# Order of projection, old MLP part and v, and where the second norm's rows are turned, in an adaLN transformer block

## The chip, the cores and the metric

The kernel runs on one core of one Trainium2 chip. Its time is device time in microseconds (us). The figure for the kernel before is the median of three runs. The engines are TensorE (PE in the profile; its weight loads are PEld), VectorE (DVE), ScalarE (ACT) and GpSimd (POOL); SyncE (SP) issues nearly all transfers here and computes nothing.

## The reference

One transformer block with adaptive layer norms, float32, for 8 sequences of 1024 tokens and D = 512, 16 heads of 32, causal attention, an MLP of width 2048:

```python
mod = silu(condition) @ Wada + bada
sh_a, sc_a, gt_a, sh_m, sc_m, gt_m = split(mod, 6, axis=1)
xn = layernorm(x, g1, be1)                                    # first norm
xm = xn * (1 + sc_a) + sh_a
x  = x + gt_a * (softmax(causal(q k^T / sqrt(32))) v @ Wproj + bproj)   # q, k, v from xm @ Wqkv
xn = layernorm(x, g2, be2)                                    # second norm
xm = xn * (1 + sc_m) + sh_m
return x + gt_m * (gelu(xm @ W1 + b1) @ W2 + b2)              # exact gelu
```

## The kernel before, in words

**Blocks and windows.** The 8192 tokens are 16 blocks of 512 rows, two a sequence; even blocks are first halves, odd ones second halves (whose attention also reads the keys and values of the half before, so it is longer). The whole kernel is one TensorE program. Attention runs block after block (`attend`). Between its matmuls the planner puts *linear work*: everything else that uses TensorE. The linear work that is to run beside block w's attention is a list of steps, `plan[w]` (the dictionary at L231 and the loop behind it); the text calls this window w. In window w, n = w - 1 is the block whose attention has just ended. Its steps are:

- `v`, `k`, `q`: the values of block w, and the keys and queries of block w + 1;
- `proj`: the output projection of block n, `project_out`. It has four tiles of 128 rows, each a sum over four 128-wide pieces of the attention's output ("steps" of a tile, in the order of the quarters of heads), with Wproj's four pieces as moving data. VectorE multiplies each tile by the gate, GpSimd or VectorE adds it to the residual rows `xr`, and then the second norm's statistics are started (`normalize`);
- `mt`: the second norm's modulation and transposition for block n (key `m`n in `modulated`, L695); `at`: the first norm's for block w + 2 (key `a`n); `load_xa`, `norm_a`: load and normalisation of that block's rows; `load_xr`: load of the rows that the residual is added to; `rows`: broadcast of gate rows;
- `u0` to `u3`: the four parts of the up projection of block n with its gelu (`up`), and `d0` to `d3`: the four parts of the down projection (`down`, L1144). The text calls d0 to d3 the first to the fourth MLP part. The parts that a window doesn't reach stay over for the next one (`late`): d2 and d3, or d1 to d3.

All linear products except the projection are done by a Strassen scheme with seven products of 256-wide halves, so each step ends in additions and subtractions on VectorE and GpSimd (`combine_out`, L193, and `either`, L158). In the second and third MLP part these give `y`, `u_d` and `v_d`; `settle` then applies the gate and adds to the residual. Before a Strassen product, differences of the halves of its input are formed (`T1` to `T4`, for `xm` at L753 and L755).

For windows 3 to 14 the order before is: late parts of block w - 2, v of block w, projection of block n, `mt`, k and q of block w + 1, u0 to u3 and d0 of block n; where w is odd, d1 and the next `at` follow in the same window. So a window after an odd one begins with d2, d3, and a window after an even one with d1, `at`, d2, d3. The two statements that matter are L253 and L263:

```python
steps = late + [("v", w)] + rows_a + [("proj", n), ("mt", n), ("k", w + 1)]
...
late = m[5:6] + at + m[6:]
```

(`m[5:6]` is d1, `m[6:]` is d2 and d3; the second statement is that of even w.) Windows 1, 2 and 15 have orders of their own.

**Turning rows.** A norm's rows lie with tokens on the partitions, and the products want features there. `by_pe` (L375) says which norms are turned on TensorE: before, all second norms, and the first norms of blocks 0 and 1. There each block takes 16 transposes of 128x128 into a PSUM bank (L735), and the modulation (scale and shift of 128x512, L739 on VectorE or L745 on ScalarE, whichever the planner holds to be free sooner) reads the bank. The other 14 first norms ("turned blocks") go another way (`turn`, L663): four VectorE transposes of 32x32 squares (L671) from the `hat` tile, which holds the normalised rows, into `xm`; one SyncE transfer of `xm` to a DRAM tile `held` (L680); four SyncE transfers back into the `hat` tile (L685), which put the squares in place; then modulation from `hat` into `xm`. There is one buffer for `hat` (`hat_tile`, L378), loaded by `load_x` for first norms.

**Attention.** For each quarter g of the heads (four heads) of a block: score units (TensorE `sc`, mask and maximum on VectorE, L1553 and L1556), weights units (`st`: minus the row maximum, then k q^T again; exponential on ScalarE into `pT`), and probabilities-times-v units (`po`). `finish` (L1682) ends a quarter: the sums of the probabilities by a product with ones (L1693), copies of sums and product to SBUF on ScalarE (`rec`, L1702, and `top`), four reciprocals of 128 columns each on VectorE (`invert`, L1711), and one multiplication on GpSimd (`quotient`, L1736), which writes the quarter's part of the attention's output over the queries `qT`. The projection of a block reads all four quarters; its last operand is that of g = 3.

**What sets the order.** Nothing is scheduled at run time: while the program is built, a planner keeps a clock for each engine (`now`), adds an estimated duration for each instruction, and keeps due times of values (`written`, `left`). Linear work runs in threads: the main one walks the plan, side threads hold what was started beside it (`at`, `mt`, tails of Strassen products). `work` advances the thread that waits least by those clocks; `step_aside` decides whether attention or linear work is next. Small jobs of VectorE, ScalarE and GpSimd (reciprocals, transposes of 32x32 squares, statistics) wait in lists and are put out once the clocks say that they are due; jobs of a second norm and of the last quarter stand first in VectorE's list. A DRAM transfer of `turn` is reckoned at 8 us each way (`HOLDING`). `costs` holds 16 transposes for each `at` and `mt`; `planned_time` makes of it the pace at which linear work is spread over a window's attention. The order so found on each engine is then fixed, and engines wait for one another by semaphores.

**Weights** come through a ring of eight SBUF tiles, in the order of the plan (`order`, `fetch`), by transfers on SyncE, which takes its instructions in order; a piece is fetched once the tile eight pieces before is released. The held tile's transfers are in the same queue.

Of the kernel before, what the change touches and what calls it, by code (L numbers as in the profile page):

```python
# [22 lines left out]
def kernel(  # L23
# [42 lines left out]
    NC = D // P  # L66
# [24 lines left out]
    NB = len(blocks)  # L91
# [3 lines left out]
    written, left = {}, {}  # L95
    shape = [None]
    pool_spans = []
    NEVER = float("inf")
# [38 lines left out]
    def note_act(ns, func, reads=(), writes=()):  # L137
        if func is not None and table[0] != func:
            table[0] = func
            ns += TABLE  # L140
        note("ACT", ns, reads, writes)

    def sooner(reads, writes, dve, act):

        t = due(reads, writes)
        return "DVE" if max(now["DVE"], t) + dve <= max(now["ACT"], t) + act else "ACT"
# [81 lines left out]
    def mlp_steps(n):  # L228
        return [("u", n, i) for i in range(NQ)] + [("d", n, part) for part in range(4)]
# [8 lines left out]
    late = []  # L238
    for w in range(1, NB):
        n = w - 1  # L240
        m = mlp_steps(n)
        even = blocks[n][1] == 0
        rows_a = [("rows", blocks[n][0], "a")] if even else []
        rows_m = [("rows", blocks[n][0], "m")] if even else []
        own = m[:1] + ([("load_xa", w + 2)] if w + 2 < NB else []) + m[1:3]
        own += [("norm_a", w + 2)] if w + 2 < NB else []
        if w == NB - 1:
            steps = late[:1] + rows_a + [("proj", n), ("mt", n)] + late[1:]
            steps += [("v", w)] + rows_m + own + m[3:5] + [("load_xr", w)] + m[5:6]
            late = m[6:]  # L250
        else:

            steps = late + [("v", w)] + rows_a + [("proj", n), ("mt", n), ("k", w + 1)]  # L253
            if w == 2:
                steps = late + [("v", w), ("k", w + 1)] + rows_a + [("proj", n), ("mt", n)]
            if w == 1:
                steps = rows_a + [("k", w + 1), ("proj", n), ("mt", n)]
            steps += [("q", w + 1)] + rows_m + own
            at = [("at", w + 2)] if w + 2 < NB else []
            if blocks[w][1] == 0:  # L260

                steps += m[3:5] + [("load_xr", w)]
                late = m[5:6] + at + m[6:]  # L263
            else:
                steps += m[3:5] + [("load_xr", w)] + m[5:6] + at
                late = m[6:]
        plan[w] = steps
    n = NB - 1
# [99 lines left out]
    at, r0 = [], 0  # L368
# [3 lines left out]
        r0 += n  # L372
    O_G1, O_BE1, O_G2, O_BE2, O_BPROJ, O_B2, O_B1, O_BADA = at

    by_pe = {f"m{n}" for n in range(NB)} | {"a0", "a1"}  # L375
    Q = P // NTT

    def hat_tile(key):  # L378
        return tmp.tile([P, NTT, D], F32, tag="hat", name=f"hat_{key}", bufs=1)

    def load_x(n):
        b, h = blocks[n]
        rows = hat_tile(f"a{n}")
        for t in range(NTT):
            some = x[b, h * TB + t * P : h * TB + (t + 1) * P, :]
            if f"a{n}" in by_pe:
                nc.sync.dma_start(rows[:, t, :], some)
            else:
                nc.sync.dma_start(rows[ts(t, Q), :, :], some.rearrange("(t i) d -> i t d", i=Q))
        return rows  # L390
# [145 lines left out]
    act_jobs = []  # L536
# [43 lines left out]
    def normalize(tiles, key, sources):  # L580

        for t in range(NTT):
            written["hat", key, t] = NEVER
        mv = small.tile([P, NTT, 2], F32, tag="mv", name=f"mv_{key}")
        rstd = small.tile([P, NTT], F32, tag="rstd", name=f"rstd_{key}")
        offset = small.tile([P, NTT], F32, tag="offset", name=f"offset_{key}")

        def statistics(t):
            st = small.tile([P, nc.vector.BN_STATS_DIM], F32, tag="st", name=f"st_{key}_{t}")
            nc.vector.bn_stats(st, tiles[:, t, :])  # L590
            nc.vector.bn_aggr(mv[:, t, :], st)
            note("DVE", 850, [sources[t]], [("mv", key)])
            if t < NTT - 1:
                return
            if alone[0]:
                root()
                for i in range(NTT):
                    apply_tile(i)
                return
            power()  # L600
            for i in range(NTT):
                act_jobs.append((lambda i=i: apply_tile(i), [("rstd", key)]))

        def root():
            nc.scalar.activation(rstd, mv[:, :, 1], AF.Sqrt, bias=eps)
            note_act(300, "sqrt", [("mv", key)], [("rstd", key)])
            nc.vector.reciprocal(rstd, rstd)
            nc.vector.scalar_tensor_tensor(offset, mv[:, :, 0], -1.0, rstd, ALU.mult, ALU.mult)
            note("DVE", 360, [("rstd", key)], [("rstd", key)], port=True)

        def power():
            nc.gpsimd.tensor_scalar(rstd, mv[:, :, 1], EPS, None, ALU.add)
            nc.gpsimd.tensor_tensor(rstd, rstd, minus_half, ALU.pow)
            nc.gpsimd.tensor_scalar(offset, mv[:, :, 0], -1.0, None, ALU.mult)
            nc.gpsimd.tensor_tensor(offset, offset, rstd, ALU.mult)
            note("POOL", 1500, [("mv", key)], [("rstd", key)])

        to = [None]

        def apply_tile(t):  # L620
            if t == 0:
                hats[key] = to[0] = hat_tile(key) if key[0] == "m" else tiles
            xh, xt = to[0][:, t, :], tiles[:, t, :]
            reads, writes = [("rstd", key)], [("hat", key, t)]
            if (key == "a0" and t % 2) if alone[0] else sooner(reads, writes, 700, 800) == "DVE":
                nc.vector.tensor_scalar(
                    xh, xt, rstd[:, t : t + 1], offset[:, t : t + 1], ALU.mult, ALU.add
                )
                note("DVE", 700, reads, writes, port=True)
            else:  # L630
                nc.scalar.activation(
                    xh, xt, AF.Identity, bias=offset[:, t : t + 1], scale=rstd[:, t : t + 1]
                )
                note_act(800, None, reads, writes)

        for t in range(NTT):
            add_job(lambda t=t: statistics(t), [sources[t]], key[0] == "m")
# [54 lines left out]
    def modulated(key, gain, shift, b, guards):  # L692
# [22 lines left out]
        at = {t: (key, t) for t in part}  # L715
        if turned:
            yield from turn(key, got, xm)
        for c in range(NC):
            if turned:
                if c:  # L720
                    yield [("turned", key)], []
                source, out = ("turned", key), xm[:, c, :].rearrange("p (a x) -> p a x", x=P)
                values = got[:, :, ts(c, P)]
                if key[0] == "m":
                    out = xm[:, c, :].rearrange("p (t a x) -> p t a x", t=2, a=NTT)
                    values = values.rearrange("p a (t x) -> p t a x", t=2)
            else:
                if c:
                    yield [("hat", key, 0)], [BANK]
                bank = lin_bank()  # L730
                source, out, values = ("l", bank), xm[:, c, :], banks[bank]
                for t in range(NTT):
                    if t:
                        yield [("hat", key, t)], []
                    nc.tensor.transpose(banks[bank][:, ts(t, P)], got[:, t, ts(c, P)], ident)  # L735
                    note_pe(TR, "whole", [("hat", key, t)], [("l", bank)])
            writes = [at["B11"], at["T1"]] if c < 2 else [at["B21"], at["B22"]]
            if sooner([source], writes, 770, 780) == "DVE":
                nc.vector.tensor_scalar(  # L739
                    out, values, gain[:, c, b : b + 1], shift[:, c, b : b + 1],  # L740
                    ALU.mult, ALU.add,
                )
                note("DVE", 770, [source], writes, port=turned)
            else:
                nc.scalar.activation(  # L745
                    out, values, AF.Identity,
                    bias=shift[:, c, b : b + 1], scale=gain[:, c, b : b + 1],
                )
                note_act(780, None, [source], writes)
            if not turned:  # L750
                live[bank] = False
            if c == 1:
                nc.vector.tensor_tensor(part["T1"], part["T1"], part["B11"], ALU.subtract)  # L753
                note("DVE", 700, [at["B11"], at["T1"]], [at["T1"]], port=True)
# [258 lines left out]
    def project_out(n):  # L1013
# [46 lines left out]
        if not last:  # L1060
            normalize(residual[n], f"m{n}", [("xr", n, t) for t in range(NTT)])
# [877 lines left out]
```

## Time and profile before

| | us |
|---|---|
| median of three runs | 3546.27 |
| lowest, highest | 3541.39, 3548.40 |
| the profiled execution, its own time | 3542.2 |
| its span (first to last instruction) | 3540.5 |

The profiled execution's mean granted TensorE clock is 0.998. A profile page gives busy time of each engine and its share of the span; then the span in 40 slices, the DMA queues, and the chain of work that ended last. After that come groups of instructions: source line, engine, operation, output<-inputs (by the program's names, buffer numbers left out) with partitions x elements, count | busy us, mean ns of one | idle time of that engine just before them and what ended most of it. Four views of the trace are used besides:

- The timeline: start in us, duration in us, engine, line, operation, operands, count (x4: four in a row, the duration is that of all four), and in brackets the idle time ahead with what ended it, where there is any. SPq is SyncE's queue.
- Waits: engine, tile and line, <- what ended the wait, then the total in us, how many, and the longest in us.
- Windows: the stretch A:B in us, its length, then busy time and number of instructions for TensorE, weight loads, VectorE, ScalarE and GpSimd, the granted clock, the DMA share and GB/s.
- One tile's or one line's instructions: count, duration in ns (shortest/median/longest), start of the first and of the last in us, forms.

### The profile page before, as it was taken

Reading aid. Unit: us, or ns where it says so; the run is one execution under the profiler, and the core shown is the slowest. Engines: PE = TensorE matmul, PEld = TensorE weight load, DVE = VectorE, ACT = ScalarE, POOL = GpSimd, SP = SyncE. Lnnn points to the kernel's source line nnn. Section 1 sums busy time; section 2 is a strip of 40 time slices with the busy share of each in tenths; the row PEclk is TensorE's granted clock in tenths of the full one; section 3 lists DMA queues with packets and bytes.
Section 4 is the critical chain, followed back from the end, with each engine's and each line's share of the span. In section 5 each row is a group of like instructions: output and inputs, shape, how many; then the busy total and the mean of one; then the engine's idle time right before and its main releaser. Section 6 shows DMA issues by size and latency. Waiting matters only on the chain.

```text
span 3540.5 us, 120499 instructions
## 1 busy us (share of the span) xinstructions
PE 3482.5 (98%) x54621; PEld 1738.0 (49%) x54621; DVE 2174.2 (61%) x2383; ACT 1190.1 (34%) x1237; POOL 2074.9 (59%) x2249
## 2 busy tenths in 40 slices
PE   8999999999999999999999999999999999999999
PEld 4444445445554555545554454544545445454445
DVE  5776675564756557565675656656566556655563
ACT  2334323352333513235232342323423234232521
POOL 2667836666376664666546675366762667526660
PEclk9999999999999999999999999999999999999999
DMA  6753434335443354524445334443344533443334
GB/s 198 245 163 103 137 117 140 111 111 156 117 148 103 110 160 117 168 85 126 142 118 159 103 115 141 124 149 107 118 132 127 156 106 119 135 126 124 100 110 140
DMA packets 319555, 465.96 MB, mean 132 GB/s; under 512 B 26300, under 2 KB 176636, under 8 KB 316996
## 3 DMA queue, kind: packets, MB, share of 16 engines
q1 hardware_dynamic: 318928, 458.22, 42.9%
q8 instruction: 430, 7.05, 0.8%
q14 instruction: 81, 0.66, 0.1%
q10 hardware_dynamic: 116, 0.03, 0.0%
HBM read 412.99 MB, written 43.06 MB: 129 GB/s over the span
## 4 chain that ended last, share of the span: by engine, by line
PE 88%; DMA 4%; DVE 3%; POOL 2%; issue 1%; ACT 1%; SPq 0%; ACTq 0%; DVEq 0%; POOLq 0%
PE bank L202 61%; PE sc L1541 8%; PE po L1672 7%; PE st L1632 7%; PE st L1620 3%; DMA w<-in_L_cond_Wproj_dram 2%; PE bank L1693 2%; PE bank L735 1%; DVE mx L1556 1%; POOL pT L1762 1%; DMA w<-in_L_cond_Wada_dram 1%; PE bank L1594 0%; POOL hT L161 0%; POOL xr L161 0%; DVE sc L1553 0%
## 5 line engine op out<-in xcount | busy, mean ns | idle before, releaser
L1762 POOL TENSOR_TENSOR pT<-pT,pT 128x256 f32<-128x256 f32 (+3 forms) x1254 | 1207.2, 998 | 347.9 <-PE po L1672 181.4
L1644 ACT ACTIVATE pT<-st 128x2048 f32<-128x2048 f32 x288 | 541.0, 1879 | 1000.5 <-PE st L1632 883.3
L202 PE MATMUL bank<-w,hT 128*32 128x256 f32 x14336 | 812.3, 380 | 1.1 <-ACT rec L1702 0.9
L1556 DVE TENSOR_REDUCE mx<-sc 128x4 f32<-128x2048 f32 (+3 forms) x384 | 666.0, 1755 | 197.7 <-PE sc L1541 191.6
L202 PEld LDWEIGHTS bank<-w,hT 128*32 128x32 f32 x14336 | 450.4, 110 | 369.2 <-issue 81.4
L202 PE MATMUL bank<-xm_m,w 128*32 128x256 f32 x8192 | 499.6, 381 | 0.0
L202 PE MATMUL bank<-t_m,w 128*32 128x256 f32 x6144 | 381.2, 380 | 0.0
L1649 POOL TENSOR_SCALAR_AFFINE_SELECT pT<-pT 128x512 f32<-128x512 f32 x256 | 168.8, 677 | 346.6 <-ACT pT L1644 344.2
L202 PEld LDWEIGHTS bank<-xm_m,w 128*32 128x32 f32 x8192 | 255.7, 110 | 224.7 <-issue 62.4
L1553 DVE TENSOR_TENSOR sc<-sc,mask 128x1024 f32<-128x1024 f32 (+1 forms) x160 | 162.9, 1018 | 319.7 <-PE sc L1541 242.5
L1541 PE MATMUL sc<-kT,qT 32*128 32x512 f32 (+3 forms) x3072 | 329.1, 520 | 1.8 <-DVE mx L1556 1.1
L1672 PE MATMUL po<-pT,v 128*32 128x512 f32 (+3 forms) x3048 | 302.9, 492 | 2.0 <-POOL pT L1649 2.0
L1632 PE MATMUL st<-qT,kT 32*128 32x512 f32 (+3 forms) x3072 | 301.0, 487 | 0.0
L202 PEld LDWEIGHTS bank<-t_m,w 128*32 128x32 f32 x6144 | 190.0, 110 | 173.3 <-issue 48.5
L202 PE MATMUL bank<-xm_a,w 128*32 128x256 f32 x3968 | 249.3, 382 | 0.0
L202 PE MATMUL bank<-w,qT 128*32 128x512 f32 x2048 | 238.2, 594 | 8.7 <-DMA w<-in_L_cond_Wproj_dram 7.2
L1711 DVE RECIPROCAL rec<-rec 128x128 f32<-128x128 f32 x256 | 225.7, 920 | 31.5 <-ACT rec L1702 31.5
L1541 PEld LDWEIGHTS sc<-kT,qT 32*128 32x128 f32 x3072 | 129.3, 183 | 179.3 <-issue 73.0
L193 DVE TENSOR_TENSOR hT<-bank,u_u 128x512 f32<-128x512 f32 x192 | 129.9, 687 | 114.1 <-PE bank L202 107.4
L202 PE MATMUL bank<-t_a,w 128*32 128x256 f32 x2944 | 188.4, 382 | 0.4 <-ACT xm_m L745 0.4
L1069 ACT ACTIVATE hT<-hT,cols 128x512 f32<-128x512 f32 x256 | 164.4, 711 | 35.5 <-DVE hT L193 35.0
L202 PEld LDWEIGHTS bank<-xm_a,w 128*32 128x32 f32 x3968 | 122.7, 110 | 105.5 <-issue 32.6
(216 smaller groups left out, 3384.6 us busy)
## 6 DMA issues: line engine op xcount, KB each, us to landing
w<-in_L_cond_W_dram SPq DMA_DIRECT2D x384, 256.0 KB
w<-kept_up_S SPq DMA_DIRECT2D x256, 256.0 KB
w<-kept_down_S SPq DMA_DIRECT2D x256, 256.0 KB
w<-kept_qkv_S SPq DMA_DIRECT2D x180, 256.0 KB
w<-in_L_cond_Wqkv_dram SPq DMA_DIRECT2D x147, 256.0 KB
hat_a<-in_x_dram SPq DMA_DIRECT2D x64, 256.0 KB
xr<-in_x_dram SPq DMA_DIRECT2D x32, 512.0 KB
w<-in_L_cond_Wproj_dram SPq DMA_DIRECT2D x64, 256.0 KB
```

The costliest lines, as they stand in the source:

```text
L193: nc.vector.tensor_tensor(out, src, other, op)
L202: nc.tensor.matmul(ps[r, :], columns, rhs, start=start, stop=stop, skip_group_check=True)
L1069: nc.scalar.activation(hT[:, i, :], hT[:, i, :], AF.Gelu, bias=cols[:, O_B1 + f : O_B1 + f + 1])
L1541: nc.tensor.matmul(sc[:, j, c0 : c0 + w], qTs[n][r, gg, ts(qt, P)], keys_of(n, kh)[r, gg, :w], start=True, stop=True, skip_group_check=True,)
L1553: nc.vector.tensor_tensor(place, place, shape_of.to_broadcast(place.shape), ALU.add)
L1556: nc.vector.tensor_reduce(maxima[n, gg][:, kh, qt, :], sc[:, :, c0 : c0 + w], axis=AX.X, op=ALU.max)
L1632: nc.tensor.matmul(st[:, j, c0 : c0 + w], kT[r, gg, ts(k % NTT, P)], qT[r, gg, TB - w :], start=False, stop=True, skip_group_check=True,)
L1644: nc.scalar.activation(pT[:, :, :used], st[:, :, :used], AF.Exp, scale=scale)
L1649: nc.gpsimd.affine_select(diagonal, diagonal, pattern=[[0, HPG], [1, P]], compare_op=ALU.is_ge, fill=0.0, base=0, channel_multiplier=-1,)
L1672: nc.tensor.matmul(po[r, TB - w :], v[:, k % NTT, g * P + j * hd : g * P + (j + 1) * hd], pT[:, j, c0 : c0 + w], start=(k == 0), stop=last ...
L1711: nc.vector.reciprocal(some, some)
L1762: nc.gpsimd.tensor_tensor(into, into, pT[:, j, c0 : c0 + w], ALU.add)
```

## The change

There are three edits.

The order of windows 3 to 14: the late parts without the last one, then the projection of block n and `mt`, and only then d3 of the block before (`late[-1:]`) and v of block w, before k and q. The projection so stands ahead of d3 and v, not behind them. For even blocks w the late list now begins with `at` and not with d1: `[at, d1, d2, d3]`.

Who turns the second norm's rows: `by_pe` keeps only `a0`, `a1`, `m0`, `m14` and `m15`. The second norms of blocks 1 to 13 go through `turn`: four VectorE transposes, `held` in DRAM and back. Two branches that were in the kernel before are thereby used: in `modulated`, the values of a turned second norm are written with the tokens in another order within each half of 256, and `down` reads the columns of the hidden layer in an order that makes up for it.

The `hat` tile is held apart: `load_x` marks it as taken, the last modulation of a first norm marks it free, and the planner puts out the normalisation of a second norm's rows only then.

```diff
--- before.py
+++ after.py
@@ -250,7 +250,7 @@
             late = m[6:]
         else:
 
-            steps = late + [("v", w)] + rows_a + [("proj", n), ("mt", n), ("k", w + 1)]
+            steps = late[:-1] + rows_a + [("proj", n), ("mt", n)] + late[-1:] + [("v", w), ("k", w + 1)]
             if w == 2:
                 steps = late + [("v", w), ("k", w + 1)] + rows_a + [("proj", n), ("mt", n)]
             if w == 1:
@@ -260,7 +260,7 @@
             if blocks[w][1] == 0:
 
                 steps += m[3:5] + [("load_xr", w)]
-                late = m[5:6] + at + m[6:]
+                late = at + m[5:]
             else:
                 steps += m[3:5] + [("load_xr", w)] + m[5:6] + at
                 late = m[6:]
@@ -372,7 +372,7 @@
         r0 += n
     O_G1, O_BE1, O_G2, O_BE2, O_BPROJ, O_B2, O_B1, O_BADA = at
 
-    by_pe = {f"m{n}" for n in range(NB)} | {"a0", "a1"}
+    by_pe = {"a0", "a1", "m0", f"m{NB - 2}", f"m{NB - 1}"}
     Q = P // NTT
 
     def hat_tile(key):
@@ -381,6 +381,7 @@
     def load_x(n):
         b, h = blocks[n]
         rows = hat_tile(f"a{n}")
+        written["hat free"] = NEVER
         for t in range(NTT):
             some = x[b, h * TB + t * P : h * TB + (t + 1) * P, :]
             if f"a{n}" in by_pe:
@@ -581,6 +582,7 @@
 
         for t in range(NTT):
             written["hat", key, t] = NEVER
+        free = ["hat free"] if key[0] == "m" else []
         mv = small.tile([P, NTT, 2], F32, tag="mv", name=f"mv_{key}")
         rstd = small.tile([P, NTT], F32, tag="rstd", name=f"rstd_{key}")
         offset = small.tile([P, NTT], F32, tag="offset", name=f"offset_{key}")
@@ -599,7 +601,7 @@
                 return
             power()
             for i in range(NTT):
-                act_jobs.append((lambda i=i: apply_tile(i), [("rstd", key)]))
+                act_jobs.append((lambda i=i: apply_tile(i), [("rstd", key), *free]))
 
         def root():
             nc.scalar.activation(rstd, mv[:, :, 1], AF.Sqrt, bias=eps)
@@ -749,6 +751,8 @@
                 note_act(780, None, [source], writes)
             if not turned:
                 live[bank] = False
+            if c == NC - 1 and key[0] == "a":
+                written["hat free"] = 0.0
             if c == 1:
                 nc.vector.tensor_tensor(part["T1"], part["T1"], part["B11"], ALU.subtract)
                 note("DVE", 700, [at["B11"], at["T1"]], [at["T1"]], port=True)
```

## The prediction

> **What bounds the kernel now.** I read the page first: busy shares, then the chain that ended last.
>
> ```profile
> span 3540.5 us, 120499 instructions
> PE 3482.5 (98%) x54621; PEld 1738.0 (49%) x54621; DVE 2174.2 (61%) x2383; ACT 1190.1 (34%) x1237; POOL 2074.9 (59%) x2249
> PE 88%; DMA 4%; DVE 3%; POOL 2%; issue 1%; ACT 1%; SPq 0%; ACTq 0%; DVEq 0%; POOLq 0%
> ```
>
> TensorE (PE) is busy 98% of the span and holds 88% of the chain. It stands still for about 58 us in all, so the kernel is a TensorE instruction stream in a fixed order: work taken off that stream is a gain, and any wait put into it is a loss, whatever the other engines do. The question is therefore what the new order makes TensorE wait for.
>
> The timeline of the stretch where block 8's attention begins (window 8: the MLP of block 6 ends, block 7 is projected) shows how such a wait is covered today. VectorE, then SyncE's queue, TensorE and GpSimd:
>
> ```profile
> 1699.40 0.69 DVE L193 TENSOR_TENSOR u_d<-bank,p_d 128x512 f32<-128x512 f32 x1 [0.42 <-PE bank L202]
> 1700.01 0.94 DVE L1711 RECIPROCAL rec<-rec 128x128 f32<-128x128 f32 x1
> 1700.86 2.43 DVE L671 STREAM_TRANSPOSE xm_a<-hat_a 128x512 f32<-128x512 f32 x4
> ...
> 1722.64 0.55 DVE L739 TENSOR_SCALAR xm_a<-hat_a,gaina,shifta 128x512 f32<-128x512 f32 x1 [1.55 <-DMA hat_a<-held_a]
> 1723.45 0.69 DVE L753 TENSOR_TENSOR xm_a<-xm_a 128x512 f32<-128x512 f32 x1 [0.26 <-ACT xm_a L745]
> 1724.87 0.69 DVE L755 TENSOR_TENSOR t_a<-xm_a 128x512 f32<-128x512 f32 x1 [0.72 <-ACT xm_a L745]
> 1725.59 0.69 DVE L158 TENSOR_TENSOR t_a<-xm_a,t_a 128x512 f32<-128x512 f32 x1
> ```
> ```profile
> 1703.53 0.42 SPq L680 DMA_DIRECT2D held_a<-xm_a  x1
> ...
> 1712.70 3.60 SPq L685 DMA_DIRECT2D hat_a<-held_a  x4
> ```
> ```profile
> 1699.80 13.56 PE L202 MATMUL bank<-w,hT 128*32 128x256 f32 x248
> 1713.18 1.91 PE L202 MATMUL bank<-w,xm_a 128*32 128x256 f32 x32
> ...
> 1723.54 1.90 PE L202 MATMUL bank<-w,qT 128*32 128x512 f32 x16
> ```
> ```profile
> 1704.14 1.73 POOL L1736 TENSOR_TENSOR qT<-top,rec 128x512 f32<-128x512 f32 x1
> ```
>
> VectorE combines the third MLP part (u_d), inverts the last quarter of block 7's softmax sums, turns block 9's first-norm rows (L671); SyncE writes them to DRAM and 9.2 us later reads them back; at 1722.64, 19.4 us after the last transpose ended, VectorE may modulate them. In that time TensorE does the fourth MLP part (1699.80 to 1713.18) and v (to 1723.54), and only then the projection (w,qT). The last quotient (GpSimd, 1704.14 to 1705.87) is finished 17 us before it is wanted. So the DRAM trip of 19 us costs nothing here, because 24 us of MLP and v lie ahead of the projection.
>
> How long that trip is, over all 14 turned blocks, from the queries by tile and ScalarE's timeline at the first and the last:
>
> ```profile
> L680 SPq DMA_DIRECT2D held_a<-xm_a x14: 338/394/1382, 130.5 to 3010.2; - x14
> ```
> ```profile
> 150.79 2.93 ACT L745 ACTIVATE xm_a<-hat_a,shifta,gaina 128x512 f32<-128x512 f32 x4 [5.94 <-DMA hat_a<-held_a]
> 3026.72 2.23 ACT L745 ACTIVATE xm_a<-hat_a,shifta,gaina 128x512 f32<-128x512 f32 x3 [5.96 <-DMA hat_a<-held_a]
> ```
>
> From issue of the write to first use: 20.3 us at the first (150.79 - 130.5), 16.5 at the last, 19.1 in the stretch above. In each, the user stood waiting for the data, so this is the trip itself.
>
> **The change, part by part.** *The transposes.* Blocks 1 to 13 lose 16 TensorE transposes each, 208 of the 224 that blocks 1 to 14 have in this stretch (TensorE busy, of L735 alone):
>
> ```profile
> 444.00:3420.00 2976.00, 39.39 (x224) 24.58 (x224) 1.00 0.42 126
> ```
>
> 39.39 x 13/14 = 36.6 us, all on the bounding engine: **-37**. In their place come 52 VectorE transposes (4 in 2.43 us above, 32 us in all on an engine that is 61% busy), modulations from SBUF, and on SyncE one write and four reads a block, 2 MB together (27 MB on 466). They run beside v, k and q, about 62 to 70 us of TensorE work between projection and first up-part, against a need of some 12 us of residual and statistics, a trip of 22 and 7 of modulations and differences: no wait for the data, except block 1, where k is ahead and only q (30 us with attention) lies between: +3 (0 to 10). The permuted token order in the down part changes no matmul count. The "hat free" condition costs nothing: ScalarE modulates the first norm's rows just ahead of normalising the second's anyway.
>
> What the 13 new trips can hold up: ScalarE stands at its modulations with exponentials and PSUM copies behind them, SyncE at its reads with weight loads behind. The existing 14 bound it:
>
> ```profile
> ACT xm_a L745 <- DMA hat_a<-held_a: 45.5, 11, 6.0
> PE bank L202 <- ACT xm_a L745: 1.1, 1, 1.1
> PE bank L202 <- DMA w<-in_L_cond_Wproj_dram: 7.2, 9, 1.5
> ```
>
> ScalarE waited 45.5 us in 11 of them, TensorE 1.1 us for all. So 13 more cost between 13 x 1.1/14 = 1 and 13 x 4.1 = 54 us; I take **+4**, near the row of the bounding engine. The 7.2 us for late Wproj pieces, queued behind the held reads, mostly go: **-5** (0 to -7).
>
> *The order.* The projection now stands ahead of the fourth MLP part and v. As built, VectorE's order in windows 6, 8, 10, 12 and 14 is: combine of the third part (in window 6 of the second), the four transposes of the next first-norm block, then **the modulation and differences of that block, and behind them the last two to four reciprocals** of the sums that the projection needs. Boundary 3 (window 4) has all reciprocals first. So at five boundaries the projection waits for the whole trip, and the cover (fourth part, v) is queued behind the projection on TensorE, where it cannot help. The costs of the steps:
>
> ```profile
> L1711 DVE RECIPROCAL rec<-rec 128x128 f32<-128x128 f32 x256 | 225.7, 920 | 31.5 <-ACT rec L1702 31.5
> L1736 POOL TENSOR_TENSOR qT<-top,rec 128x512 f32<-128x512 f32 x61 | 80.1, 1314 | 49.9 <-DVE rec L1711 49.8
> L158 DVE TENSOR_TENSOR v_d<-v_d,u_d 128x512 f32<-128x512 f32 x4 | 3.3, 814 | 0.1
> L158 DVE TENSOR_TENSOR hT<-hT 128x1024 f32<-128x1024 f32 x16 | 26.0, 1652 | 0.0
> L1553 DVE TENSOR_TENSOR sc<-sc,mask 128x1024 f32<-128x1024 f32 x96 | 118.3, 1232 | 187.2 <-PE sc L1541 121.0 <-issue 31.3 <-ACT rec L1702 26.0
> L1556 DVE TENSOR_REDUCE mx<-sc 128x4 f32<-128x1536 f32 x64 | 112.5, 1758 | 2.2
> L1556 DVE TENSOR_REDUCE mx<-sc 128x4 f32<-128x512 f32 x64 | 43.6, 681 | 0.0
> ```
>
> Window 8 (block 7), counted from the last matmul of the third part: combine 0.69, add to v_d 0.81, transposes 2.43, trip 19.35 (1703.29 to 1722.64), modulation and differences 3.64 (1722.64 to 1726.28), two reciprocals 1.84, quotient 1.31: 30.1 us. TensorE's work in that time, from the rows of its timeline:
>
> ```profile
> 1506.95 0.40 PE L1620 MATMUL st<-mrow,minus_ones 32*128 32x256 bf16 x8
> 1507.17 1.03 PE L1632 MATMUL st<-qT,kT 32*128 32x256 f32 x16
> 1508.14 1.07 PE L1672 MATMUL po<-pT,v 128*32 128x384 f32 x16
> ...
> 1517.14 1.04 PE L1693 MATMUL bank<-pT,ones 128*32 128x512 f32 x8
> ...
> 1518.97 1.14 PE L1541 MATMUL sc<-kT,qT 32*128 32x512 f32 x8
> ```
>
> one probabilities-times-v unit 1.0, the sums 1.0, one score unit 1.1, one weights unit 1.2, and three of the four steps of the first projection tile, which need the earlier quarters only, at half of 1.8 each (2.7): 7 us. Stall: 30 - 7 = **23 us**. The others by the same count: window 10 has two small operations more ahead of the transposes (gate and residual, 2.3) and 1.3 us more cover: 24. Window 12 has in addition four reciprocals (+1.8) and a masked score unit behind the differences (1.23 + 1.76 + 0.68 = 3.7), cover 11: 27. Window 14 likewise, 38 against 15: 23. Window 6 turns after the y combine, two subtractions (3.3) and the gate, and has three reciprocals: 35 against 15: 20. Sum **+117**. Window 4 lacks only the plain chain of reciprocals and quotient: **+4**. Of the odd windows, 11 and 13 run out of linear work before their projection and lose some 2 and 5 us: **+7**; the others have 14 to 27 us of MLP in between.
>
> *After a stall the clock is low.* TensorE's one long pause, at the tail, in windows by 5 us (busy TensorE, granted clock):
>
> ```profile
> 3431.00:3436.00 5.00, 1.36 (x5) 0.80 (x5) 2.68 (x8) 2.27 (x4) 0.00 (x0) 0.78 0.60 198
> 3436.00:3441.00 5.00, 5.00 (x40) 3.39 (x43) 2.89 (x4) 2.33 (x3) 0.82 (x1) 0.54 0.00 0
> 3441.00:3450.00 9.00, 9.00 (x176) 5.01 (x168) 2.08 (x3) 1.17 (x2) 5.92 (x5) 1.00 0.45 131
> ```
>
> After 3.6 us of pause it ran 5 us at 0.54, which loses 2.3 us; five stalls: **+12**.
>
> Sum: -37 - 5 + 3 + 4 + 117 + 4 + 7 + 12 = +105 us on the profiled run of 3542.2 us (span 3540.5): 3647. The median of the three runs, 3546.27, is 4 us above that run: **3650 us**.
>
> Two places of the Trainium skill. The page "DMA: Bandwidth & Descriptors" (section Bandwidth) has 6.15 us for a 1 MB transfer, so by an estimate from it write and read take 12.3 us; the five stalls would be 7 us shorter and the sum 3615. The trace does not agree (16.5 to 20.3). The page "VectorE: DVE Perf Modes" (Rules for kernel authors) speaks against the change: it would transpose 128x128 on TensorE where a PSUM destination will do, since VectorE turns only 32x32 blocks; that is what makes the DRAM trip necessary. By that rule the 13 blocks would stay, and the reordering alone would give 3650 + 37 - 7 = 3680 us; that 2.4 us of VectorE replace 2.8 us of the bounding engine is what the trace puts against it.
>
> **The rivals.** *A, faster:* the projection does not wait for the trip. If the reciprocals ran ahead of the modulation, as at 1700.01 above and in window 4, each boundary would lose nothing more: -42 + 3 + 4 + 4 + 7 = -24, **3522 us**. It decides at the place of those two to four reciprocals in VectorE's order; with them behind, the trip would have to shrink from 19 us to nearly nothing. Against it stands that engines take their instructions in order. *B, heavier:* the 13 new trips block ScalarE by 4.1 us each and this reaches TensorE: +50, **3700 us**. For it: ScalarE's 45.5 us; against: TensorE's 1.1. *C, lighter:* with TensorE standing and few weights moving, the trip is at the shortest row, 16.5: 5 x 2.6 less, **3637 us**. (The skill's transfer time above would carry this to 3615.) *D, the moves cancel* at some 3546: would need stalls of about 6 us, for which no row speaks.
>
> **How the numbers follow.** Main 0.70 (3615 to 3690), A 0.05, B 0.14, C 0.08, D 0.03. The range 3600 to 3705 leaves out A, D and the far end of B. Faster by over 0.2% 0.05, within it (what a measurement here can tell from none) 0.03, slower 0.92.
>
> **What would show it.** In the profile after: TensorE waits of 20 to 28 us ahead of the projection's matmuls (w,qT) in five windows, every second one, released by GpSimd's quotient or by reciprocals; VectorE and ScalarE idle there for hat_a<-held_a; granted clock low after each; L735's successor with 80 transposes. Wrong if TensorE's busy share stays at 98%, if the pauses stand ahead of the up part instead (the second norm's own trip), or if they are spread over all 13 blocks (B).

## The result, and the profile after

| | before | after |
|---|---|---|
| median, us | 3545.6 (four runs) | 3656.1 (four runs) |
| lowest, highest | 3541.39, 3548.40 | 3653.79, 3658.59 |
| ratio to before, 95% interval | | 1.0309 (1.0294 to 1.0325) |
| span of the profiled run | 3540.5 | 3652.1 |
| mean granted clock | 0.998 | 0.981 |

The page after: span, then busy time, share and instructions of each engine.

```profile
span 3652.1 us, 120374 instructions
PE 3496.2 (96%) x54413; PEld 1735.6 (48%) x54413; DVE 2198.9 (60%) x2441; ACT 1194.1 (33%) x1244; POOL 2091.4 (57%) x2256
```

TensorE has 208 matmul records fewer and is busy 13.7 us longer (3482.5 before). Its pauses, the gaps in its timeline added up (the wait for the first matmul included), grew from 54 to 152 us. So the 111.6 us of span are about 98 us of standing and 14 us of busy time; since the transposes took some 37 busy us away, matmuls that are left ran slower by about 50 us in sum.

The timeline after, at the boundary where block 7's projection begins (the stretch that the prediction shows of before): TensorE, VectorE, SyncE's queue, GpSimd. A bracket gives the idle time ahead and what ended it.

```profile
1712.04 1.05 PE L1676 MATMUL po<-pT,v 128*32 128x384 f32 x16
1712.90 2.71 PE L1697 MATMUL bank<-pT,ones 128*32 128x512 f32 x8
1715.54 1.15 PE L1545 MATMUL sc<-kT,qT 32*128 32x384 f32 x16
1720.51 0.61 PE L1624 MATMUL st<-mrow,minus_ones 32*128 32x384 bf16 x8 [3.81 <-DVE mx L1560]
1720.91 2.03 PE L1636 MATMUL st<-qT,kT 32*128 32x384 f32 x16
1722.87 0.62 PE L1598 MATMUL bank<-ident_b,mcols 128*32 128x128 bf16 x16
1723.27 3.88 PE L202 MATMUL bank<-w,qT 128*32 128x512 f32 x24
1735.81 5.73 PE L202 MATMUL bank<-w,qT 128*32 128x512 f32 x36 [8.66 <-POOL qT L1740]
```
```profile
1713.71 2.48 DVE L673 STREAM_TRANSPOSE xm_a<-hat_a 128x512 f32<-128x512 f32 x4
1716.83 1.23 DVE L1557 TENSOR_TENSOR sc<-sc,mask 128x1024 f32<-128x1024 f32 x1 [0.64 <-PE sc L1545]
1718.10 2.35 DVE L1560 TENSOR_REDUCE mx<-sc 128x4 f32<-128x1536 f32 x2
1720.37 1.75 DVE L1715 RECIPROCAL rec<-rec 128x128 f32<-128x128 f32 x2
1728.70 0.55 DVE L741 TENSOR_SCALAR xm_a<-hat_a,gaina,shifta 128x512 f32<-128x512 f32 x1 [6.58 <-DMA hat_a<-held_a]
...
1732.34 1.75 DVE L1715 RECIPROCAL rec<-rec 128x128 f32<-128x128 f32 x2
```
```profile
1716.22 0.32 SPq L682 DMA_DIRECT2D held_a<-xm_a  x1
1721.05 1.74 SPq L687 DMA_DIRECT2D hat_a<-held_a  x4
```
```profile
1734.17 1.58 POOL L1740 TENSOR_TENSOR qT<-top,rec 128x512 f32<-128x512 f32 x1 [0.63 <-DVE rec L1715]
```

VectorE turns block 9's rows, inverts two of the four quarters, then stands 6.58 us for rows that are on their way through DRAM. Only behind the modulation of these come the other two reciprocals (1732.34); GpSimd's quotient follows (1734.17), and TensorE goes on with the projection at 1735.81 after 8.66 us of standing. Three things differ from what was forecast. The wait ahead of the projection is 8.66 us, not 23. The trip, from the last VectorE transpose (1713.71 + 2.48) to first use (1728.70), is 12.5 us, not 19.4. And there is a second pause ahead of the projection: from 1712.04 on TensorE has only attention to do, no MLP matmul lies between, and it waits 3.81 us for a maximum.

The same stretch in windows of 5 us: length, then busy time and instructions of TensorE, weight loads, VectorE, ScalarE and GpSimd, granted clock, DMA share, GB/s.

```profile
1715.00:1720.00 5.00, 1.69 (x19) 0.72 (x16) 4.33 (x6) 1.07 (x2) 2.60 (x3) 0.87 0.52 211
1720.00:1725.00 5.00, 4.49 (x52) 2.18 (x56) 2.12 (x3) 1.91 (x2) 1.00 (x4) 0.50 0.55 128
1725.00:1730.00 5.00, 2.15 (x20) 0.39 (x12) 0.95 (x2) 1.70 (x3) 1.22 (x2) 0.95 0.42 83
1730.00:1735.00 5.00, 0.00 (x0) 0.00 (x0) 4.25 (x7) 0.97 (x2) 2.59 (x2) 0.74 0.00 0
1735.00:1740.00 5.00, 4.19 (x24) 1.03 (x28) 1.99 (x2) 0.00 (x0) 4.88 (x4) 0.58 0.00 0
```

After the pause of 3.81 us the clock is at 0.50 for 5 us, after that of 8.66 us at 0.58. A shorter pause is enough: at block 5's boundary TensorE stood 1.95 us, and the next 3.4 us have 0.50.

```profile
1273.70 0.40 PE L1624 MATMUL st<-mrow,minus_ones 32*128 32x384 bf16 x8 [1.95 <-DVE mx L1560]
```
```profile
1275.00:1278.40 3.40, 3.40 (x36) 1.15 (x36) 0.10 (x1) 2.35 (x2) 3.24 (x3) 0.50 0.98 219
```

The Trainium skill's page "TensorE: Matmul & The Clock Gate" (section on the HAM clock gate) says that about 3.4 us of idling halve the clock, and that about 3.4 us of work bring it back. This trace agrees with the page in the granted 0.50 and in the 3.4 us that it lasts at block 5's boundary; the pause ahead of it, 1.95 us, is shorter than the page's idle time, and here the measurement decides.

Where the time went, by stretches: from the first matmul of the up parts (xm_m,w in TensorE's timeline) of block n - 1 to that of block n. The three kernels on the right are explained below.

| n | before | after | order_over | after_paced | d3first_paced |
|---|---|---|---|---|---|
| 5 | 216.4 | 239.8 | 238.2 | 230.5 | 226.1 |
| 6 | 216.9 | 204.9 | 211.1 | 203.6 | 205.2 |
| 7 | 216.5 | 242.1 | 240.1 | 230.4 | 226.1 |
| 8 | 214.0 | 202.9 | 209.6 | 203.0 | 203.9 |
| 9 | 218.6 | 247.5 | 241.4 | 230.8 | 226.2 |
| 10 | 217.7 | 211.5 | 223.2 | 203.9 | 205.8 |
| 11 | 216.0 | 249.3 | 241.5 | 232.0 | 226.1 |
| 12 | 218.8 | 214.3 | 215.1 | 203.8 | 205.2 |
| 13 | 215.4 | 235.9 | 236.5 | 239.2 | 226.1 |
| 14 | 163.6 | 179.5 | 185.6 | 168.2 | 168.4 |

That odd stretches are longer and even ones shorter than before is work that moved across a stretch's ends; all four new kernels have it. What is lost shows between them: after stands above the last column by 13.7, 16.0, 21.3, 23.2 and 9.8 us at the odd boundaries, growing up to block 11's, and by 5.7, 9.1 and 11.1 us at those of blocks 10, 12 and 14.

### The profile page after: what moved, and what is told of

It is laid out like the page before. It is cut to its first block, busy times and chain, and to the rows that moved or that the text cites. A ratio compares the mean times of both kernels' runs of the same rounds, so it can differ in the third digit from the quotient of the medians.

```text
span 3652.1 us, 120374 instructions
## 1 busy us (share of the span) xinstructions
PE 3496.2 (96%) x54413; PEld 1735.6 (48%) x54413; DVE 2198.9 (60%) x2441; ACT 1194.1 (33%) x1244; POOL 2091.4 (57%) x2256
## 5 line engine op out<-in xcount | busy, mean ns | idle before, releaser
L1766 POOL TENSOR_TENSOR pT<-pT,pT 128x256 f32<-128x256 f32 (+3 forms) x1254 | 1220.3, 1008 | 433.0 <-PE po L1676 247.7
L1560 DVE TENSOR_REDUCE mx<-sc 128x4 f32<-128x2048 f32 (+3 forms) x380 | 656.3, 1748 | 234.1 <-PE sc L1545 227.8
L1636 PE MATMUL st<-qT,kT 32*128 32x512 f32 (+3 forms) x3072 | 309.0, 497 | 0.0
L202 PE MATMUL bank<-w,qT 128*32 128x512 f32 x2048 | 246.6, 632 | 28.3 <-POOL qT L1740 27.6
L202 PEld LDWEIGHTS bank<-xm_a,w 128*32 128x32 f32 x3968 | 124.1, 110 | 111.6 <-issue 29.2
L1740 POOL TENSOR_TENSOR qT<-top,rec 128x512 f32<-128x512 f32 x61 | 79.9, 1310 | 166.5 <-DVE rec L1715 166.5
```

The lines of the kernel that those rows point to most:

```text
L202: nc.tensor.matmul(ps[r, :], columns, rhs, start=start, stop=stop, skip_group_check=True)
L1560: nc.vector.tensor_reduce(maxima[n, gg][:, kh, qt, :], sc[:, :, c0 : c0 + w], axis=AX.X, op=ALU.max)
L1636: nc.tensor.matmul(st[:, j, c0 : c0 + w], kT[r, gg, ts(k % NTT, P)], qT[r, gg, TB - w :], start=False, stop=True, skip_group_check=True,)
L1740: nc.gpsimd.tensor_tensor(qTs[n][:, g, :], top, rec, ALU.mult)
L1766: nc.gpsimd.tensor_tensor(into, into, pT[:, j, c0 : c0 + w], ALU.add)
```

## The experiments

Each was timed against the kernel before on the same chip (medians of 3544.4, 3544.7 and 3545.2 us in the three groups, each on another chip; a difference between kernels of two groups carries that spread).

**order_alone, turn_alone: the two halves of the change.** The first has the changed kernel's order and `by_pe` as before; the second the changed kernel's `by_pe`, and L253 and L263 as before. Both keep the `hat free` condition.

```diff
# order_alone
-    by_pe = {"a0", "a1", "m0", f"m{NB - 2}", f"m{NB - 1}"}
+    by_pe = {f"m{n}" for n in range(NB)} | {"a0", "a1"}
# turn_alone
-            steps = late[:-1] + rows_a + [("proj", n), ("mt", n)] + late[-1:] + [("v", w), ("k", w + 1)]
+            steps = late + [("v", w)] + rows_a + [("proj", n), ("mt", n), ("k", w + 1)]
-                late = at + m[5:]
+                late = m[5:6] + at + m[6:]
```

> The changed kernel with the two order statements of the kernel before; the second norms of blocks 1 to 13 are still turned through DRAM. Theory T (the loss sits at five boundaries, where the last reciprocals stand behind the modulation of rows that are on their way through DRAM, ahead of an uncovered projection): those losses go, the 208 TensorE transposes stay away (33 us of TensorE's sequence), the trips cost something where only k and q lie between projection and first up part: 3515 to 3540 us. Rival R2 (the 13 new trips hold up ScalarE and SyncE, and that is the loss): slower than before, 3570 to 3640.

Measured: 3585.7 us, ratio 1.0113 (1.0098 to 1.0128). T misses by 45 us and more; the number is in R2's range.

> The changed kernel's order, with all second norms turned on TensorE as before. T: the stalls stay and 33 us of transposes come back, about 3690 (3675 to 3705). R2: without the 13 trips most of the loss goes, 3550 to 3600.

Measured: 3561.2 us, 1.0040 (1.0025 to 1.0054). T falls by 130 us: where no second norm is turned through DRAM the new order costs 17 us, not 145. This number, too, lies in R2's range; order_over below decides against R2 for the changed kernel's loss.

The two halves cost 17 and 41 us alone, both at once 111: nearly half of the loss (53 us) belongs to neither alone. Turning's own 41 us are seen in TensorE's timeline of turn_alone, at the end of q (t_a, xm_a) and the beginning of the up parts (xm_m), and in SyncE's queue:

```profile
1372.11 1.91 PE L202 MATMUL bank<-t_a,w 128*32 128x256 f32 x32
1373.95 1.14 PE L1545 MATMUL sc<-kT,qT 32*128 32x512 f32 x8
1377.50 1.14 PE L1545 MATMUL sc<-kT,qT 32*128 32x512 f32 x8 [2.41 <-DVE mx L1560]
1381.06 0.62 PE L1624 MATMUL st<-mrow,minus_ones 32*128 32x512 bf16 x4 [2.41 <-DVE mx L1560]
...
1387.62 1.93 PE L202 MATMUL bank<-xm_m,w 128*32 128x256 f32 x32
```
```profile
1368.74 0.32 SPq L682 DMA_DIRECT2D held_m<-xm_m  x1
...
1374.57 1.83 SPq L687 DMA_DIRECT2D hat_m<-held_m  x4
```

q is done at 1374, the second norm's rows are still on their way through DRAM and the modulation behind it, and until 1387.62 TensorE has attention only. Nothing in TensorE's row says "DMA": the wait shows as `mx`, because a score unit without other work beside it stands until its maximum is taken (2.41 us, twice). In the old order k and q alone don't cover the second norm's trip; this, not ScalarE or SyncE held up (R2), is what the rows show at this boundary. The largest single piece lies at block 1, where only q is in between: its stretch takes 276.3 us, before 256.9.

**rec_first: the reciprocals ahead of the modulation.** The lines are new in `modulated`, ahead of its loop over c:

```diff
+        if key in ("a7", "a9", "a11", "a13", "a15"):
+            yield [("turned", key), ("attended", int(key[1:]) - 2)], []
```

> The changed kernel, in which the modulation of the first-norm rows of blocks 7, 9, 11, 13 and 15 waits in the planner until the last quotient of two blocks before has been put out; TensorE's and SyncE's order is that of the changed kernel, instruction by instruction, only VectorE, ScalarE and GpSimd change places around the five boundaries. T: the five boundaries lost 105 us against full pitch; what stays is the plain chain of reciprocals and quotient, 4 to 7 us each: 3570 to 3590. Rival R1 (the projection's place ahead of the fourth part and v is the loss, whatever VectorE does first): 3635 to 3660.

Measured: 3624.2 us, 1.0223 (1.0207 to 1.0238). Both ranges miss: 32 us come back, not 80 and not none. VectorE's and TensorE's timeline at the same boundary:

```profile
1712.64 2.35 DVE L1562 TENSOR_REDUCE mx<-sc 128x4 f32<-128x1536 f32 x2
1714.92 3.38 DVE L1717 RECIPROCAL rec<-rec 128x128 f32<-128x128 f32 x4
```
```profile
1715.06 0.61 PE L1626 MATMUL st<-mrow,minus_ones 32*128 32x384 bf16 x8 [3.82 <-DVE mx L1562]
...
1722.40 7.93 PE L202 MATMUL bank<-w,qT 128*32 128x512 f32 x72 [0.79 <-POOL qT L1742]
```

All four reciprocals are through, the 8.66 us have shrunk to 0.79, and the pause of 3.8 us for the maximum with its slow clock is still there. The order on VectorE, which the prediction made nearly the whole loss, is about a third of it (32 of 111 us).

**hop: the trip made longer.** In `turn`, between the write and the reads:

```diff
+        if key in ("a7", "a9", "a11", "a13", "a15"):
+            hop = kept.tile([P, NTT * D], F32, tag="hop", name=f"hop_{key}")
+            nc.sync.dma_start(hop, held)
+            held = hop
```

> The changed kernel, in which the rows of the same five blocks go through a second DRAM tile before they are read back (one 1 MB transfer more each); nothing else moves. T: the trip is on the path at all five, so each boundary loses the hop's length, by the 3.9 us between write and read and the 7.7 us from read to use that the changed kernel shows there 4 to 8 us: 3675 to 3697. R1 and R2: the trip of the first norm's rows is not what the projection waits for, 3650 to 3662.

Measured: 3673.5 us, 1.0363 (1.0345 to 1.0380), 17 us above the changed kernel: just under T's range. The stretches n = 5, 7 and 11 grew by 5.4, 7.1 and 5.8 us, those of 9 and 13 by 0.9 and 1.7. VectorE's row at block 7's boundary shows the longer trip:

```profile
1717.01 2.48 DVE L673 STREAM_TRANSPOSE xm_a<-hat_a 128x512 f32<-128x512 f32 x4
...
1738.51 0.55 DVE L745 TENSOR_SCALAR xm_a<-hat_a,gaina,shifta 128x512 f32<-128x512 f32 x1 [13.08 <-DMA hat_a<-hop_a]
```

19.0 us in place of 12.5, and the stretch is 7.1 us longer. So the trip sets the end at three boundaries; at two others something else was as late.

**after_paced, order_over: the pace.** What neither half has alone can come from the planner. It sets a window's pace as `planned_time` over attention's need, and puts linear work first as long as it lags behind that pace. `planned_time` counts 16 transposes (16 x 108 ns, 1.7 us) for each `mt`. The changed kernel no longer makes them on TensorE in 13 windows, so linear work is asked for faster than attention goes, and is used up before a block's attention ends. What is left then, attention's last units, reciprocals and the next rows' trip, stands bare. The first kernel mends the pace in the changed kernel; the second puts the same excess, in all windows, into order_alone, which turns every second norm on TensorE.

```diff
# after_paced
-        return parts + sum(costs.get(step[0], 0) for step in plan[w])
+        return parts + sum(costs.get(step[0], 0) for step in plan[w] if step[0] != "mt" or f"m{step[1]}" in by_pe)
# order_over, on order_alone
-    costs = {"at": 16 * TR, "mt": 16 * TR, "gates": 4 * MM, "mod": 32 * TR}
+    costs = {"at": 16 * TR, "mt": 32 * TR, "gates": 4 * MM, "mod": 32 * TR}
```

> The changed kernel, in which the pace of the linear work counts the 16 transposes of an mt step (16 x 108 ns = 1.7 us a window) only where TensorE makes them. Theory D (the pace is too high by that much, so linear work runs ahead, is used up before a block's attention ends, and at the boundary attention's last units, reciprocals and the trip stand bare): each of the five boundaries falls to the 5 to 7 us that they lose in the kernel with the order alone, 3560 to 3590 us. Rival X (the trips and their queues cost it, whatever the pace): 3640 to 3660.

Measured: 3563.5 us, 1.0056 (1.0041 to 1.0071). D holds: one number in the planner gives back 93 of 111 us.

> The kernel with the order alone, all second norms on TensorE, no instruction added or taken away, but the pace counts 32 transposes for an mt step where TensorE makes 16: the same 1.7 us a window too much that the changed kernel has. D: the loss of the changed kernel comes without a turned row: 3561 plus 60 to 110, 3620 to 3670 us. X: 3550 to 3575.

Measured: 3671.4 us, 1.0361 (1.0344 to 1.0378): 110 us above order_alone, just over D's range, with no second norm turned through DRAM. X falls, and with it R2. TensorE's timeline of after_paced and then of order_over, again up to block 7's projection:

```profile
1700.05 1.15 PE L1545 MATMUL sc<-kT,qT 32*128 32x384 f32 x16
1701.12 5.39 PE L202 MATMUL bank<-w,hT 128*32 128x256 f32 x96
1706.44 0.40 PE L1624 MATMUL st<-mrow,minus_ones 32*128 32x384 bf16 x8
1706.67 1.09 PE L1636 MATMUL st<-qT,kT 32*128 32x384 f32 x16
1707.69 2.80 PE L202 MATMUL bank<-w,hT 128*32 128x256 f32 x48
...
1716.59 4.05 PE L202 MATMUL bank<-w,qT 128*32 128x512 f32 x20 [3.30 <-POOL qT L1740]
```
```profile
1719.85 3.16 PE L1697 MATMUL bank<-pT,ones 128*32 128x512 f32 x8 [2.81 <-POOL pT L1766]
1722.94 1.40 PE L1545 MATMUL sc<-kT,qT 32*128 32x384 f32 x16
1728.16 0.61 PE L1624 MATMUL st<-mrow,minus_ones 32*128 32x384 bf16 x8 [3.83 <-DVE mx L1560]
...
1740.17 1.08 PE L202 MATMUL bank<-w,qT 128*32 128x512 f32 x4 [5.10 <-POOL qT L1740]
```

With the pace mended, MLP matmuls (w,hT) still lie between score and weights unit and ahead of the projection; the third part ends last. With the excess they are gone. VectorE's order follows. In after_paced the reciprocals come first again and the transposes behind them:

```profile
1711.16 3.38 DVE L1715 RECIPROCAL rec<-rec 128x128 f32<-128x128 f32 x4
1714.46 2.43 DVE L673 STREAM_TRANSPOSE xm_a<-hat_a 128x512 f32<-128x512 f32 x4
```

In order_over two reciprocals stand behind the modulation, as in the changed kernel:

```profile
1733.05 0.57 DVE L741 TENSOR_SCALAR xm_a<-hat_a,gaina,shifta 128x512 f32<-128x512 f32 x1 [3.27 <-issue]
...
1736.70 1.76 DVE L1715 RECIPROCAL rec<-rec 128x128 f32<-128x128 f32 x2
```

So the order that the prediction read is itself an effect of the pace. That linear work is used up early shows at every boundary. The time from the end of the last MLP matmul (w,hT) to the projection's first (w,qT), in which TensorE has attention only, in us, from the timelines ("0" is under 0.1):

| block projected | 5 | 7 | 9 | 10 | 11 | 12 | 13 | 14 | 15 |
|---|---|---|---|---|---|---|---|---|---|
| after | 3.6 | 11.0 | 20.1 | 9.8 | 32.5 | 14.9 | 30.8 | 15.2 | 14.1 |
| after_paced | 0 | 0 | 0 | 0 | 0 | 0 | 1.4 | 1.1 | 0 |
| order_alone | 0 | 0 | 0 | 0 | 0 | 0 | 1.4 | 1.1 | 0 |
| order_over | 9.5 | 16.1 | 18.2 | 21.3 | 28.5 | 14.0 | 32.6 | 22.6 | 13.4 |

It grows along the odd blocks up to block 11, as an excess that adds up from window to window would make it.

**turn_paced.** turn_alone with the line of after_paced.

> The second norm's rows turned through DRAM in the old order (3585.7 us), with the pace mended as above. That kernel lost 5 to 10 us a window, most of it between the end of q and the first up part, where the rows are still on their way. Theory U (k and q alone don't cover the second norm's trip): the pace changes little, 3575 to 3595. If it was the pace there too: 3515 to 3545.

Measured: 3601.2 us, 1.0165 (1.0150 to 1.0180). That is 6 us above U's range. It wasn't the pace in this order; mending it even cost 15 us, which U did not foresee and which stays unexplained.

**d3first_paced and its kin: a version that is faster than both.** d3 goes ahead of the projection again and v behind it, and the pace counts transposes of `at` and `mt` only where TensorE makes them (L263 as before).

```diff
-            steps = late[:-1] + rows_a + [("proj", n), ("mt", n)] + late[-1:] + [("v", w), ("k", w + 1)]
+            steps = late + rows_a + [("proj", n), ("mt", n), ("v", w), ("k", w + 1)]
-        return parts + sum(costs.get(step[0], 0) for step in plan[w])
+        return parts + sum(costs.get(step[0], 0) for step in plan[w] if step[0] not in ("at", "mt") or ("a" if step[0] == "at" else "m") + str(step[1]) in by_pe)
```

> Rows turned through DRAM as in the change, late MLP parts all ahead of the projection, v behind it with k and q, and the pace counts no transposes that TensorE doesn't make (for at and mt). By D and U together: d3 lies ahead of the projection and gives the reciprocals their time, v, k and q cover the second norm's trip, and the 33 us of transposes are gained less some 10 for block 1: 3515 to 3535, faster than before. If trips as such cost (X): 3560 to 3600.

Measured: 3531.6 us, 0.9965 (0.9952 to 0.9979): faster than before.

d3first_debt has this order with the old pace:

> The faster kernel's order, rows turned through DRAM, but with the pace as in the changed kernel (16 transposes too many for each mt and each at). D (the debt uses up the linear work before attention's end): the loss comes back, though d3 lies ahead of the projection: 3560 to 3600. If d3 ahead of the projection is cover enough: 3528 to 3538.

Measured: 3557.2 us, 1.0033 (1.0021 to 1.0045). 26 us for the pace, against 93 in the changed kernel's order, and somewhat under D's lower end. TensorE's timeline has attention only ahead of the projections of blocks 13, 14 and 15 (13.5, 15.2 and 14.1 us) and 1.4 us or less ahead of the others; that d3 ahead of the projection is what holds it off so long was not tested apart.

d3_pe_p2 has order and pace of d3first_paced with `by_pe` as before:

> The faster kernel (late MLP parts, projection, v, k, q; pace mended for at and mt) with all second norms on TensorE. If turning still gains what the transposes took, less block 1's loss of some 10 us: 3531.6 + 33 - 10, 3550 to 3560 us. If the order alone made the gain and the trips give back the transposes: 3530 to 3540.

Measured: 3545.1 us, 0.9998 (0.9989 to 1.0007): the same as before. It lies between the two ranges: turning gains 13.5 us here.

d3p_m1 is d3first_paced with block 1's second norm on TensorE (`"m1"` added to `by_pe`):

> The faster kernel with block 1's second norm left on TensorE. There only q lies between projection and first up part, and against full pitch that stretch lost 16 us where the kernel before lost 8; the transposes come back with 2.5 us. Theory U (uncovered trip of block 1): 3531.6 - 8 + 2.5, 3523 to 3529. If block 1's trip is not what costs there: 3532 to 3536.

Measured: 3523.3 us, 0.9939 (0.9926 to 0.9951). Its page:

```profile
span 3521.5 us, 120371 instructions
PE 3458.3 (98%) x54429; PEld 1711.9 (49%) x54429; DVE 2217.5 (63%) x2415; ACT 1211.6 (34%) x1256; POOL 2097.5 (60%) x2262
```

TensorE is at 98% again and has 24 us of busy time less than before. Leaving block 1 out gains 8.2 us though 2.5 us of transposes come back, so, by this estimate, its uncovered trip cost some 11 us.

## Why the prediction was right in its number and wrong in a step

3650 us were forecast, 3656.1 measured; the size came out, partly by luck: terms that were wrong made up for one another.

*Right:* TensorE's stream is the bound, waits put into it are losses, and the change is slower by about the forecast size. The pauses lie at the boundaries of blocks 5, 7, 9, 11 and 13, with reciprocals behind the modulation at each and the covering work behind the projection. Taking away that order (rec_first) and lengthening the trip (hop) moved the time the way that it says.

*The step that failed* is that these stalls belong to the reordering, "+117" from the order as built, and with it the 3680 us given for the reordering alone. That kernel takes 3561. The order in which VectorE's work came out was read as a property of the new plan. It was a result of the plan together with a pace that still counted transposes that TensorE had lost: after_paced (-93 us) and order_over (+110) show it from both sides. The prediction read the order correctly and did not ask why it was so.

Nor are the stalls of the forecast kind. Its sign was a wait of 20 to 28 us for the quotient ahead of the projection in five windows. The timeline after has 9.3, 8.7, 5.0, 0.3 and nothing there: 23 of 73 us of pauses. The rest stands inside attention, which has no linear work beside it any more: 29 us for maxima, 11 for GpSimd's work on `pT`, 8 for ScalarE's exponential, and under 2 for `mcols`.

*The terms.* Five stalls: +117 as standing time; the pauses over 1 us at these boundaries add up to 73 (11.2, 12.5, 15.5, 20.0, 13.6). The trip in them was taken as 19 us; at block 7's boundary it is 12.5. The Trainium skill's transfer time on the page "DMA: Bandwidth & Descriptors" (section Bandwidth), which the prediction set aside, comes by its estimate to 12.3 us for write and read; the five trips after, 11.6 to 12.5 us, agree. Beside them at most one weight piece was fetched; in the same place before it were 9 to 11 pieces, and the trips took 16.5 to 19.1 us. So rival C's condition of few weights held, and its 16.5 was still too long. Low clock: +12 was too small; there is more than one pause at a boundary. (The row that it was taken from has a pause of 2.87 us and shorter ones; 3.6 us is all the idle time of that window.) Taking each matmul form's usual start-to-start time of before off the timeline after leaves 105 us lost at the five boundaries, so about 32 us beside the 73 of standing, for the low clock and for gaps under 1 us. Together 105 against 129 forecast. The same count gives some 17 us for the stretches of blocks 10 and 12 beyond what they lost before (+7 forecast), 5 to 6 for block 3 (+4), and some 13 for those of blocks 14 and 15, which had no term. Block 1's trip: +3 (0 to 10) against some 11 in d3p_m1. Transposes: -37 by busy time; in the order with cover, turning 13 blocks gained 13.5 us net, or some 24 without block 1's loss. What took the rest was not separated.

*The rivals.* A (3522, reciprocals first): its order was made in rec_first, which takes 3624. It was wrong in that the modulation is not the only thing that TensorE stands for there; attention without linear work beside it stands too. B (the 13 trips block ScalarE, 4.1 us each): ScalarE waits 8.5 us in all for second-norm rows in turn_alone, and in d3first_paced for none that the view shows. For held first-norm rows it waits there eight times as long as before (45.5 us), and the kernel is faster. Total, number and longest:

```profile
ACT xm_a L747 <- DMA hat_a<-held_a: 357.9, 13, 36.9
```

So such waits need not cost anything. In the changed kernel one did, though on a first norm's trip and not on the 13 new ones: at block 11's boundary ScalarE stood 19.66 us for held rows, the exponential queued behind them came late, and TensorE waited 7.75 us for it:

```profile
2631.39 2.22 ACT L747 ACTIVATE xm_a<-hat_a,shifta,gaina 128x512 f32<-128x512 f32 x3 [19.66 <-DMA hat_a<-held_a]
2633.52 1.85 ACT L1648 ACTIVATE pT<-st 128x2048 f32<-128x2048 f32 x1
2635.43 2.09 PE L1545 MATMUL sc<-kT,qT 32*128 32x384 f32 x16 [7.75 <-ACT pT L1648]
```

D (the moves cancel) did not come; by the prediction's own terms its stalls would have been just under 5 us, not 6 (24 us over five boundaries, low clock left out).

## What to carry to other kernels

When work moves off the bounding engine, mend every place that still counts it there: a build-time planner with a stale cost can lose more than the move gains, and the loss shows up far from it, as a bad order. Then time it: in two orders the mended cost gained 93 and 26 us here, in a third (turn_paced) it lost 15. When an order looks bad, ask what made it so before giving it a price as if it were fixed. A long transfer needs independent work of the bounding engine behind its start, and the consumer's other inputs need some ahead of it: here one MLP part ahead of the projection, and v, k and q behind it. (For block 1, with only q behind it, the transposes on TensorE were the better choice, by 8.2 us.)

## What was not expected of the hardware

From issue of the write to first use, the round trip of 1 MB through DRAM took 11.6 to 12.5 us at the five boundaries, with no weight piece or one fetched beside it, and 16.5 to 19.1 us in the same place of the kernel before, with 9 to 11 pieces in the same queue, by the same instructions. It is not the standing of TensorE as such that makes it short: in after_paced, whose boundaries lose far less, it took 11.6 to 12.1 us beside none to three pieces. And a pause of only 1.95 us already brought the clock to 0.50 for 3.4 us, so a boundary with several short pauses can run slow after each: at block 9's the clock was at 0.50 from 2163 to 2169, from 2173 to 2179 and again from 2186.5 to 2189.5.
